# An attention block and two quantised convolutions on one core: a later second convolution, per-chunk statistics, halved first units

## The chip, the cores and the metric

The kernel runs on one core of one Trainium2 chip. The metric is device time in microseconds (us); lower is better. Names such as L1125 are line numbers of the kernel before the change. PE is the matrix engine, DVE the vector engine, ACT the scalar engine, POOL the GpSimd engine, and SP the engine that issues most of the DMAs here.

## The reference, cut to what matters

The input is `x`, 4 images of 128 channels by 128 x 128 pixels, float32. Two layers follow each other.

```python
# layer 0, for each image
tok  = windows of 16x16 pixels, stride 14              # 81 windows
tok  = attention(layernorm(tok) @ w_qkv) @ w_out + b_out + tok
xf   = overlap-average of the windows                   # 128 channels
ym   = layernorm(xf) @ w_p0 + b_p0                      # 256 channels
ym   = depthwise_conv_5x5(ym)
ym   = batchnorm(ym) over images and pixels             # needs every ym first
y    = gelu(gelu(ym)) @ w_p2 + b_p2 + xf                # 128 channels
# layer 1
q    = round(15 * clip(y, 0, 1))
c1   = conv3x3(q, 4-bit w1);  n1 = batchnorm(c1)        # needs every c1 first
q    = round(15 * clip(n1, 0, 1))
c2   = conv3x3(q, 4-bit w2);  n2 = batchnorm(c2)        # needs every c2 first
out  = n2 + y
```

Each of the three batch norms needs the statistics of a whole tensor before its result can be used, so the kernel has four stages with a joint between each two.

## The kernel before, in words

Everything is in one function, `layers`. It is built twice, once for ordinary scores and once (`safe`) under a condition at the end; with these inputs only the first build runs.

**First stage** (to about 2280 us): attention, the first layer norm, the projections and most of the depthwise convolution, in an order of steps written out by hand for the PE, ACT, DVE and SP queues (`tc.manual_schedule`). A planner-free loop over 36 bands of windows puts one band's scores, the next band's layer norm and the previous band's projection beside each other.

**Tail of the depthwise convolution** (`conv_rest`, L644 to L712): the last two row groups of image 3 are convolved in eight chunks of 32 channels, `step(k)` for k from 0 to 7. A chunk is 192 matmuls, two ACT copies out of PSUM (L686), eight `bn_stats` on DVE (L690) and four stores to the DRAM tensor `cv_d`. This call stands outside the hand-made order, so the scheduler of the language puts its instructions in order.

**Depthwise statistics** (L1025 to L1055): 64 `bn_aggr` (L1034) reduce the per-unit statistics `st0` to a mean and a variance per group; a few small DVE operations, eight products with `quad` (L1044) and four one-column matmuls (L1046) add up the partitions; `affine` makes the scale `sc0` and the shift `sh0`. This block too is ordered by the scheduler.

From here on the work goes in 64 *units*: a unit is 8 rows of one image, 1024 pixels, numbered image by image, so that image 3 is units 48 to 63.

**Gelu stage** (`gelu_stage`, from L1148). In step n SP loads unit n+2 (`cv`, 1 MB, then `xfl`, 0.5 MB), ACT does the two gelus of unit n+1 (L1171 twice, L1174), PE does the projection of unit n (L1183, eight matmuls), DVE and POOL make `y`, clip it and quantise it into the padded fp8 image `q1` (L1191, L1195, L1201, L1137), and PE does the first 3x3 convolution of unit n-2 (L1125, 18 matmuls: two halves of 4 rows by 9 taps). DVE takes its statistics (L1133), and ACT copies the result to SBUF (L1207); it goes to DRAM (`c1_d`) except for image 3, which stays in the SBUF tile `c1_s`.

**Second convolution** (`last_stages`, first loop, L1269 to L1287). In step n: ACT scales unit n and applies relu in place (L1277), DVE clips and rounds (L1278) and writes the fp8 integers into `q1` (L1137), PE convolves unit n-2 (L1125), DVE takes its statistics (L1133). For image 3 the result is also copied by ACT into `c1_s` (L1285), in the place from which the unit's input had been read. Each engine takes these in the order of the program, and PSUM has four buffers for results (`ps_d`). At n = 63 the statistics of the units 0 to 59 are aggregated (`most`, L1000), and after the loop the rest (`rest`, L1009).

**Last stage** (L1290 to L1300): the units of images 0 to 2 are convolved a second time, ACT applies the batch norm (L1294), DVE adds `y` (L1295), SP stores the result and loads the next `y`; for image 3 the kept result is used.

Of the kernel before, what the change touches and what calls it, by code (L numbers as in the profile page):

```python
# [8 lines left out]
F32 = mybir.dt.float32  # L9
F8 = mybir.dt.float8e4  # L10
AF = mybir.ActivationFunctionType
# [35 lines left out]
def layers(  # L47
# [49 lines left out]
    c1_d = [dram.tile([P, P * P], F32, name=f"c1_d{b}") for b in range(B - 1)]  # L97
    id_d = [dram.tile([P, P * P], F32, name=f"id_d{b}") for b in range(B)]

    def vector(v, name):  # L100
        n = v.shape[0] // P
        t = const.tile([P, n], F32, name=name)
        nc.sync.dma_start(out=t, in_=v.rearrange("(h p) -> p h", p=P))
        return t

# [27 lines left out]
    with (  # L133
# [36 lines left out]
    st0 = sctx.enter_context(tc.tile_pool(name=f"st0_{tag}", bufs=1)).tile(  # L170
        [P, NCK, 2, 4, len(units), 6], F32, name="st0"
    )


    with ExitStack() as actx:
# [468 lines left out]
        def conv_rest(n, w_t, u_t, c_t):  # L644

            b, g0, ng = units[n]
            early = 5
            at = GR + 2  # L650

            def load(k, a, z, g, m):
                for half in range(2):
                    ch = 32 * k + 16 * half
                    nc.sync.dma_start(
                        out=U[k][64 * half + 2 * a : 64 * half + 2 * z, g : g + m].rearrange(
                            "p g c x -> p g (c x)"
                        ),
                        in_=input_of(b, g0 + g, m, ch, 16, a, z),
                    )  # L660

            U = [u_t.tile([P, ng, 16, CW], F32, name=f"u{k}") for k in range(NCK)]
            W = [w_t.tile([P, 3, 16, 32], F32, name=f"w{k}") for k in range(NCK)]
            for k in range(NCK):
                weights(W[k], k, 0, 2, nc.gpsimd.dma_start)
            for k in range(early):
                load(k, 0, at, 0, 1)

            def late(k):
                if k < early:  # L670
                    load(k, 0, at, 1, 1)
                    load(k, at, GR + 4, 0, ng)
                else:
                    load(k, 0, GR, 0, ng)
                    load(k, GR, GR + 4, 0, ng)

            def step(k):
                sc = ps_s.tile([P, 2, 2, NT], F32, name=f"sc{k % 2}")
                pc = [
                    sc[:, half].rearrange("p a n -> p (a n)").rearrange("p (j g x) -> p j g x", j=4, g=ng)  # L680
                    for half in range(2)
                ]
                depthwise(pc, W[k], U[k], 16)
                for half in range(2):
                    cv = c_t.tile([P, 4, ng, CW], F32, name=f"c{half}")
                    nc.scalar.copy(  # L686
                        cv.rearrange("p j g x -> p (j g x)"), pc[half].rearrange("p j g x -> p (j g x)")
                    )
                    for j in range(4):
                        nc.vector.bn_stats(  # L690
                            st0[:, k, half, j, n, :], cv[:, j].rearrange("p g x -> p (g x)")
                        )
                    engine = (nc.sync, nc.scalar)[half]
                    for g in range(ng):
                        engine.dma_start(
                            out=bass.AP(
                                cv_d[b].tensor,
                                cv_d[b][g0 + g, 32 * k + 16 * half, 0:1].offset,
                                [[CW, P], [4 * GR * P, 4], [1, CW]],
                            ),  # L700
                            in_=cv[:, :, g],
                        )

            def run_all():
                for k in range(4):
                    late(k)
                for k in range(NCK):
                    step(k)
                    if k + 4 < NCK:
                        late(k + 4)  # L710

            return run_all  # L712
# [311 lines left out]

    mv0 = const.tile([P, 2, 2], F32, name="mv0")  # L1025
    with (
        tc.tile_pool(name=f"bn0_{tag}", bufs=1) as bn0,
        tc.tile_pool(name=f"ps_q_{tag}", bufs=1, space=PSUM) as ps_q,
    ):
        nk = NCK * 2 * 4  # L1030
        mv = bn0.tile([P, 2, nk], F32, name="mvp")
        flat = st0.rearrange("p k a j n s -> p (k a j) (n s)")
        for k in range(nk):
            nc.vector.bn_aggr(mv[:, :, k], flat[:, k, :])  # L1034
# [5 lines left out]
        pq = ps_q.tile([P, 2, 2], F32, name="pq")  # L1040
        for m in range(2):
            ex = bn0.tile([P, nk, 4], F32, name=f"ex{m}")
            for q in range(4):
                nc.vector.tensor_scalar(ex[:, :, q], mv[:, m, :], quad[:, q : q + 1], None, ALU.mult)  # L1044
            for h in range(2):
                nc.tensor.matmul(  # L1046
                    pq[:, m, h : h + 1],
                    ex.rearrange("p k q -> p (k q)")[:, h * P : (h + 1) * P], all1,
                    start=True, stop=True,
                )  # L1050
# [4 lines left out]
    sc0, sh0 = affine(mv0[:, 0, :], mv0[:, 1, :], 2, bng, bnb, "0")  # L1055

    sctx.close()

# [89 lines left out]
    def gelu_stage():  # L1148
        with (
# [7 lines left out]
            def load(n):  # L1157
                b, k = units[n]
                cv = ld.tile([P, 2, U], F32, name="cv")
                nc.sync.dma_start(  # L1160
                    out=cv,
                    in_=cv_d[b][k // 2].rearrange("(h p) n -> p h n", p=P)[:, :, pixels(k % 2)],
                )
                xf = ld.tile([P, U], F32, name="xfl")
                nc.sync.dma_start(out=xf, in_=xf_d[b][:, pixels(k)])
                loaded[n] = cv, xf

            def gelus(n):
                cv = loaded[n][0]
                for h in range(2):  # L1170
                    nc.scalar.activation(  # L1171
                        cv[:, h], cv[:, h], AF.Gelu, bias=sh0[:, h : h + 1], scale=sc0[:, h : h + 1]
                    )
                nc.scalar.activation(cv, cv, AF.Gelu)  # L1174

            def second_projection(n):
                b, k = units[n]
# [32 lines left out]

            for n in range(2):
                load(n)
            gelus(0)
            before1()
            before2()
            for n in range(len(units) + 2):
                if n + 2 < len(units):
                    load(n + 2)
                while stores:
# [12 lines left out]
                if n == len(units) - 1:  # L1232
                    most1()
# [5 lines left out]
    def last_stages():  # L1239
        with (  # L1240
# [25 lines left out]
            for n in range(2):  # L1266
                load_first(n)
            sc1, sh1 = rest1()
            for n in range(len(units) + 2):  # L1269
                if n + 2 < len(units):  # L1270
                    load_first(n + 2)
                if n % 4 == 3 and n // 4 < 8:
# [1 line left out]
                if n < len(units):  # L1274
                    b, k = units[n]
                    a = firsts.pop(n)
                    nc.scalar.activation(a, a, AF.Relu, bias=sh1, scale=sc1)  # L1277
                    nc.vector.tensor_scalar(a, a, 15.0, ROUND, ALU.min, ALU.add)  # L1278
                    to_int(rows_in(q1[b], k), a)
                if n >= 2:  # L1280
                    b, k = units[n - 2]
                    pc = conv3x3(ps_d, n - 2, wq[1])
                    stats_of(st2, n - 2, pc)
                    if b == B - 1:
                        nc.scalar.copy(c1_s[:, pixels(k)], pc.rearrange("p h n -> p (h n)"))  # L1285
                if n == len(units) - 1:
# [64 lines left out]
```

## Time and profile before

| what | value |
|---|---|
| time, median of 3 runs | 3292.92 us (3278.27, 3292.92, 3293.81) |
| time of the profiled execution | 3289.4 us |
| its span, first to last instruction | 3287.5 us |
| mean granted PE clock | 0.959 |
| PE busy | 3089.1 us, 94% of the span |
| DVE, ACT, POOL busy | 61%, 61%, 25% |
| DMA moved | 682.75 MB, mean 208 GB/s |
| chain that ended last, PE's share | 76% |

The busy time is summed over the whole span, and the four stages have different limits: in the page's 40 slices PE is at 9 tenths nearly everywhere, and drops to 8, 8 and 4 around 2270 to 2350 us, the tail of the depthwise convolution and its statistics. The question for a change of this sort is therefore not how busy an engine is, but at which places PE waits, and for whom.

### The profile page before, as it was taken

The numbers are of one execution on the slowest core, as the hardware profiler recorded it, in microseconds if no ns is written. First come the engines' busy times: TensorE is split into PE (matmuls) and PEld (weight loads), VectorE is DVE, ScalarE is ACT, GpSimd is POOL, SyncE is SP. The second block draws the span as 40 slices with busy tenths as digits, with TensorE's granted clock in tenths as the row PEclk, the third lists the DMA queues.
The fourth block names the chain that finished last, engine by engine and source line by source line (L and its number), as shares of the span: only waits on it lengthen the run. The fifth ranks groups of instructions, "written<-read, shape, count | busy, mean of one in ns | idle before, by whom it ended". The sixth has DMA issues, their size and how long they took to land.

```text
span 3287.5 us, 75680 instructions
## 1 busy us (share of the span) xinstructions
PE 3089.1 (94%) x30922; PEld 1540.7 (47%) x30922; DVE 2018.0 (61%) x3247; ACT 1989.9 (61%) x2654; POOL 836.3 (25%) x1058
## 2 busy tenths in 40 slices
PE   7999999999999999999999998884899999999998
PEld 3555554544444554444444444553544444444343
DVE  4877887676766667666655564442455555666543
ACT  5777776777777776777656564432477767433443
POOL 3444443333333333333222232211111111000000
PEclk8999999999999999999999998876699999999999
DMA  4555677898886788886888888757899999452398
GB/s 92 133 164 166 173 181 177 195 212 196 204 202 163 192 208 204 195 208 166 190 200 207 202 195 201 192 160 186 256 356 358 358 358 300 150 167 70 101 359 308
DMA packets 810450, 682.75 MB, mean 208 GB/s; under 512 B 581014, under 2 KB 696047, under 8 KB 810095
## 3 DMA queue, kind: packets, MB, share of 16 engines
q1 hardware_dynamic: 799471, 671.26, 75.2%
q8 instruction: 246, 4.03, 0.5%
q0 software_dynamic: 1024, 3.93, 0.5%
q10 hardware_dynamic: 9600, 2.62, 0.4%
q14 instruction: 109, 0.89, 0.1%
HBM read 410.81 MB, written 270.81 MB: 207 GB/s over the span
## 4 chain that ended last, share of the span: by engine, by line
PE 76%; DMA 9%; ACT 5%; issue 4%; DVE 3%; SPq 2%; POOL 0%; ACTq 0%; DVEq 0%; POOLq 0%
PE pc L1125 19%; PE pm L566 9%; PE sc L749 9%; PE po L812 8%; PE pm L459 7%; PE pb L1183 6%; PE pm L527 5%; PE pm L735 4%; PE po L820 3%; DMA y_d<-y 3%; PE pm L358 3%; PE pm L511 3%; DMA u<-y_d 2%; ACT pt L757 1%; DMA xn<-row 1%
## 5 line engine op out<-in xcount | busy, mean ns | idle before, releaser
L832 DVE RECIPROCAL rd<-po 128x256 f32<-128x256 f32 x324 | 569.3, 1757 | 451.6 <-PE po L820 446.5
L1125 PE MATMUL pc<-q,wq 128*128 128x512 fp8e4 x3168 | 701.4, 381 | 14.3 <-DVE q L1137 14.3
L757 ACT ACTIVATE pt<-sc 128x1024 f32<-128x1024 f32 x648 | 627.8, 1024 | 129.1 <-PE sc L749 64.7
L767 POOL TENSOR_TENSOR sm<-pt 128x512 f32<-128x512 f32 x324 | 412.6, 1274 | 1052.8 <-ACT pt L757 748.8
L1125 PEld LDWEIGHTS <-wq 128*128 128x128 fp8e4 x3168 | 308.9, 98 | 417.2 <-issue 49.5
L749 PE MATMUL sc<-q,kr 32*128 32x256 f32 x5184 | 403.6, 414 | 18.9 <-ACT pt L757 18.8
L566 PE MATMUL pm<-u,w 40*32 40x504 f32 (+5 forms) x7680 | 369.2, 504 | 37.2 <-DMA u<-y_d 24.9
L749 PEld LDWEIGHTS sc<-q,kr 32*128 32x128 f32 x5184 | 249.1, 190 | 258.4 <-issue 166.4
L812 PE MATMUL po<-pt,v 128*32 128x256 f32 x5184 | 360.1, 397 | 7.8 <-DVE part L836 7.0
L527 PE MATMUL pm<-xn,wp 128*128 128x512 f32 (+1 forms) x576 | 251.9, 568 | 57.6 <-DVE xn L389 29.4
L613 ACT COPY c<-pm 128x512 f32<-128x512 f32 (+1 forms) x256 | 132.2, 562 | 269.1 <-PE pm L566 257.6
L532 ACT ACTIVATE y<-pm,bp 128x512 f32<-128x512 f32 (+1 forms) x288 | 182.9, 640 | 165.9 <-DMA y_d<-y 86.9
L459 PE MATMUL pm<-xn,wqkv 128*128 128x512 f32 (+1 forms) x576 | 251.9, 566 | 11.2 <-DVE xn L389 7.7
L767 DVE TENSOR_TENSOR sm<-pt 128x512 f32<-128x512 f32 x324 | 243.3, 751 | 27.4 <-ACT pt L757 27.4
L566 PEld LDWEIGHTS pm<-u,w 40*32 40x32 f32 x7680 | 147.0, 112 | 218.7 <-issue 163.5
L617 DVE BATCH_NORM_STATS2 st<-c 128x6 f32<-128x512 f32 (+2 forms) x320 | 160.8, 550 | 138.5 <-ACT c L613 137.9
L1183 PE MATMUL pb<-cv,wp 128*128 128x512 f32 x512 | 231.6, 596 | 6.8 <-ACT cv L1174 6.8
L812 PEld LDWEIGHTS po<-pt,v 128*32 128x32 f32 x5184 | 139.4, 111 | 181.2 <-issue 107.5
L1133 DVE BATCH_NORM_STATS2 st<-pc 128x6 f32<-128x512 f32 x256 | 165.6, 689 | 66.8 <-PE pc L1125 66.8
L820 PE MATMUL po<-sm,ones 128*32 128x256 f32 x2592 | 205.7, 388 | 0.0
L735 PE MATMUL pm<-wqkv,yr 128*128 128x128 f32 x1296 | 193.0, 290 | 0.0
L735 PEld LDWEIGHTS pm<-wqkv,yr 128*128 128x128 f32 x1296 | 158.7, 191 | 68.0 <-issue 44.3
(149 smaller groups left out, 3424.9 us busy)
## 6 DMA issues: line engine op xcount, KB each, us to landing
cv<-cv_d SPq DMA_DIRECT2D x64, 1024.0 KB
u<-y_d SPq DMA_DIRECT2D x230, 256.0 KB
cv_d<-c SPq DMA_DIRECT2D x192, 256.0 KB
xn<-row SPq DMA_DIRECT2D x80, 512.0 KB
y_d<-y SPq DMA_DIRECT2D x160, 256.0 KB
xfl<-xf_d SPq DMA_DIRECT2D x64, 512.0 KB
id_d<-y SPq DMA_DIRECT2D x64, 512.0 KB
idt<-id_d SPq DMA_DIRECT2D x64, 512.0 KB
```

The costliest lines, as they stand in the source:

```text
L459: nc.tensor.matmul(pm[:, : n * P], wqkv[:, m * P : (m + 1) * P], held["xn"][hh], start=True, stop=True,)
L527: nc.tensor.matmul(pm[:, : n * P], wp0[:, h, :], held["xn"][hh], start=True, stop=True)
L566: nc.tensor.matmul(outs[half][32 * q : 32 * q + 32, j, :, a:z], wt[hs, s, c, :], ut[hs, :, c, a + s - 1 : z + s - 1], start=(s == 1), stop ...
L735: nc.tensor.matmul(pv[:, m, c, :], region(yr, j + m)[:, c * P : (c + 1) * P], wqkv[:, 2 * P :], start=True, stop=True,)
L749: nc.tensor.matmul(sc[h // 2][:, h % 2, kc, :].rearrange("p (r c) -> p r c", c=RS), region(kr, j)[hs, kc * P : (kc + 1) * P], queries(j, h ...
L757: nc.scalar.activation(pt, sc[p], AF.Exp)
L767: add(sm, pt[:, :, 0, :], pt[:, :, 1, :], ALU.add)
L812: nc.tensor.matmul(po[hs, 0, :], v[:, kc, hs], pt[h // 2][:, h % 2, kc, :], start=(kc == 0), stop=(kc == 1),)
L820: nc.tensor.matmul(po[hs, 1, :], ones, sm[h // 2][:, h % 2, :], start=True, stop=True)
L832: nc.vector.reciprocal(rd, po[:, 1, :])
L1125: nc.tensor.matmul(pc[:, h], w[:, t, :], q1[b][:, r + dy : r + dy + RB, dx : dx + P], start=(t == 0), stop=(t == 8),)
L1183: nc.tensor.matmul(pb[:, m], wp2[:, h, :], cv[:, h, px], start=(h == 0), stop=(h == 1))
```

## The change

It has five parts.

1. The small vectors of weights (`vector`, L100) become slices of one tile `vectors` instead of a tile each.
2. The 64 `bn_aggr` are written into the loop of `conv_rest`, eight behind each chunk, and write to a tile `mvp` that is allocated beside `st0`. The statistics block is put under the hand-made order, and its eight products with `quad` become one DVE instruction over 512 elements with repeated operands.
3. The gelus of unit 0 are done in two halves of 512 pixels, each with its three ACT instructions.
4. In the gelu stage the first two loads of `cv` go ahead of the first two loads of `xfl`.
5. In the second convolution the first unit is quantised in two halves of 4 rows, and the convolution of unit n-3 (before: n-2) stands in step n.

```diff
     def vector(v, name):
         n = v.shape[0] // P
-        t = const.tile([P, n], F32, name=name)
+        t = vectors[:, used[0] : used[0] + n]
+        used[0] += n
...
+    def chunk_stats(k):
+        flat = st0[:, k].rearrange("p a j n s -> p (a j) (n s)")
+        for m in range(8):
+            nc.vector.bn_aggr(mvp[:, :, 8 * k + m], flat[:, m, :])
...
                 for k in range(NCK):
                     step(k)
+                    chunk_stats(k)
...
     with (
+        nullcontext() if safe else tc.manual_schedule(engines=MANUAL),
...
-        for k in range(nk):
-            nc.vector.bn_aggr(mv[:, :, k], flat[:, k, :])
...
+        nc.vector.tensor_tensor(
+            mq[1],
+            bass.AP(mq[0].tensor, mq[0].offset, [*mq[0].ap, [0, 4]]),
+            bass.AP(quad.tensor, quad.offset, [quad.ap[0], [0, 2 * nk], quad.ap[1]]),
+            ALU.mult,
+        )
         for m in range(2):
-            ex = bn0.tile([P, nk, 4], F32, name=f"ex{m}")
-            for q in range(4):
-                nc.vector.tensor_scalar(ex[:, :, q], mv[:, m, :], quad[:, q : q + 1], None, ALU.mult)
...
             def gelus(n):
-                cv = loaded[n][0]
-                for h in range(2):
...
-                nc.scalar.activation(cv, cv, AF.Gelu)
+                for px in (slice(0, U // 2), slice(U // 2, U)) if n == 0 else (slice(0, U),):
+                    cv = loaded[n][0][:, :, px]
+                    for h in range(2):
...
+                    nc.scalar.activation(cv, cv, AF.Gelu)
...
             for n in range(2):
                 load(n)
+            for n in range(2):
+                load_xf(n)
...
-            for n in range(len(units) + 2):
+            for n in range(len(units) + 3):
...
-                    nc.scalar.activation(a, a, AF.Relu, bias=sh1, scale=sc1)
-                    nc.vector.tensor_scalar(a, a, 15.0, ROUND, ALU.min, ALU.add)
-                    to_int(rows_in(q1[b], k), a)
-                if n >= 2:
-                    b, k = units[n - 2]
-                    pc = conv3x3(ps_d, n - 2, wq[1])
-                    stats_of(st2, n - 2, pc)
+                    for h in (slice(0, RB), slice(RB, 2 * RB)) if n == 0 else (slice(0, 2 * RB),):
+                        px = slice(h.start * P, h.stop * P)
+                        nc.scalar.activation(a[:, px], a[:, px], AF.Relu, bias=sh1, scale=sc1)
+                        nc.vector.tensor_scalar(a[:, px], a[:, px], 15.0, ROUND, ALU.min, ALU.add)
+                        to_int(rows_in(q1[b], k)[:, h], a[:, px])
+                if n >= 3:
+                    b, k = units[n - 3]
+                    pc = conv3x3(ps_d, n - 3, wq[1])
+                    stats_of(st2, n - 3, pc)
```

More of the change, by code (lines that the diff above doesn't have):

```diff
@@ L98, in layers @@
     id_d = [dram.tile([P, P * P], F32, name=f"id_d{b}") for b in range(B)]
+    vectors, used = const.tile([P, 24], F32, name="vectors"), [0]
     def vector(v, name):
         n = v.shape[0] // P
-        t = const.tile([P, n], F32, name=name)
+        t = vectors[:, used[0] : used[0] + n]
+        used[0] += n
         nc.sync.dma_start(out=t, in_=v.rearrange("(h p) -> p h", p=P))
@@ L169, in layers @@
     sctx = ctx.enter_context(ExitStack())
-    st0 = sctx.enter_context(tc.tile_pool(name=f"st0_{tag}", bufs=1)).tile(
-        [P, NCK, 2, 4, len(units), 6], F32, name="st0"
-    )
+    stp = sctx.enter_context(tc.tile_pool(name=f"st0_{tag}", bufs=1))
+    st0 = stp.tile([P, NCK, 2, 4, len(units), 6], F32, name="st0")
+    mvp = stp.tile([P, 2, NCK * 2 * 4], F32, name="mvp")
+    def chunk_stats(k):
+        flat = st0[:, k].rearrange("p a j n s -> p (a j) (n s)")
+        for m in range(8):
+            nc.vector.bn_aggr(mvp[:, :, 8 * k + m], flat[:, m, :])
     with ExitStack() as actx:
@@ L1030, in layers @@
         nk = NCK * 2 * 4
-        mv = bn0.tile([P, 2, nk], F32, name="mvp")
-        flat = st0.rearrange("p k a j n s -> p (k a j) (n s)")
-        for k in range(nk):
-            nc.vector.bn_aggr(mv[:, :, k], flat[:, k, :])
+        mv = mvp
         sq = bn0.tile([P, nk], F32, name="sqp")
@@ L1040, in layers @@
         pq = ps_q.tile([P, 2, 2], F32, name="pq")
+        ex = bn0.tile([P, 2, nk, 4], F32, name="ex")
+        mq = [mv.rearrange("p m k -> p (m k)"), ex.rearrange("p m k q -> p (m k) q")]
+        nc.vector.tensor_tensor(
[4 more added lines that the diff above has]
+        )
         for m in range(2):
-            ex = bn0.tile([P, nk, 4], F32, name=f"ex{m}")
-            for q in range(4):
-                nc.vector.tensor_scalar(ex[:, :, q], mv[:, m, :], quad[:, q : q + 1], None, ALU.mult)
             for h in range(2):
@@ L1047, in layers @@
                     pq[:, m, h : h + 1],
[L1048 removed]
+                    ex[:, m].rearrange("p k q -> p (k q)")[:, h * P : (h + 1) * P], all1,
                     start=True, stop=True,
@@ L1054, in layers @@
         nc.vector.tensor_tensor(mv0[:, 1, :], mv0[:, 1, :], sq0, ALU.subtract)
-    sc0, sh0 = affine(mv0[:, 0, :], mv0[:, 1, :], 2, bng, bnb, "0")
+        sc0, sh0 = affine(mv0[:, 0, :], mv0[:, 1, :], 2, bng, bnb, "0")
     sctx.close()
@@ L1163, in load, with load_xf @@
                 )
+                loaded[n] = [cv]
+            def load_xf(n):
+                b, k = units[n]
                 xf = ld.tile([P, U], F32, name="xfl")
                 nc.sync.dma_start(out=xf, in_=xf_d[b][:, pixels(k)])
-                loaded[n] = cv, xf
+                loaded[n].append(xf)
             def gelus(n):
-                cv = loaded[n][0]
-                for h in range(2):
[L1171 to L1174, printed above, removed]
+                for px in (slice(0, U // 2), slice(U // 2, U)) if n == 0 else (slice(0, U),):
+                    cv = loaded[n][0][:, :, px]
+                    for h in range(2):
+                        nc.scalar.activation(
+                            cv[:, h], cv[:, h], AF.Gelu, bias=sh0[:, h : h + 1], scale=sc0[:, h : h + 1]
+                        )
+                    nc.scalar.activation(cv, cv, AF.Gelu)
             def second_projection(n):
@@ L1218, in gelu_stage @@
                     load(n + 2)
+                    load_xf(n + 2)
                 while stores:
```

## The prediction

> **What bounds the kernel now.** I read the page's slices first, for where PE falls below 9 tenths; then PE in order of time over those slices; then the chain of waits there.
>
> The slices of the page:
>
> ```profile
> PE   7999999999999999999999998884899999999998
> PEclk8999999999999999999999998876699999999999
> DMA  4555677898886788886888888757899999452398
> ```
>
> Each digit is 82 us. Nothing in the change touches the first 26 slices except where small vectors lie, so look right of the 4 (slice 29): the statistics block and the start of the gelu stage. Then the second convolution in order of time, on PE (start, length, work, idle before it and who ended it):
>
> ```profile
> 2809.98 11.88 PE L1125 MATMUL pc<-q,wq 128*128 128x512 fp8e4 x54
> 2827.88 212.53 PE L1125 MATMUL pc<-q,wq 128*128 128x512 fp8e4 x969 [6.02 <-DVE q L1137]
> 3041.25 4.07 PE L1125 MATMUL pc<-q,wq 128*128 128x512 fp8e4 x18 [0.83 <-DVE q L1137]
> 3046.15 4.07 PE L1125 MATMUL pc<-q,wq 128*128 128x512 fp8e4 x18 [0.83 <-DVE q L1137]
> ...
> 3080.43 4.07 PE L1125 MATMUL pc<-q,wq 128*128 128x512 fp8e4 x18 [0.83 <-DVE q L1137]
> 3085.33 14.92 PE L1125 MATMUL pc<-q,wq 128*128 128x512 fp8e4 x68 [0.83 <-DVE q L1137]
> ```
>
> PE is unbroken to 3040 and then waits once per unit for DVE. The chain of waits from 3015 to 3092 shows why; here is one round of it:
>
> ```profile
> 3027.79 1.01 ACT c_s L1285
> 3028.80 1.15 ACT c_s L1277
> 3029.95 0.02 issue
> 3029.97 0.70 DVE c_s L1278
> 3030.68 0.02 issue
> 3030.70 0.70 DVE q L1137
> 3031.40 1.21 DVE st L1133 x2
> ```
>
> This is a ring without PE: statistics, copy to `c1_s`, relu of the next unit (behind the copy in ACT's queue), rounding, integers, and then the next statistics (behind them in DVE's queue). One round is 4.90 us (3032.69 less 3027.79, the next copy's start), while PE needs 3.91 for 18 matmuls. So image 3 costs PE 0.99 us a unit: ten gaps from 3041 to 3085, 9.9 us.
>
> The other two places, first DVE in the convolution's tail and then ACT at the gelu stage's start:
>
> ```profile
> 2328.84 1.65 DVE L690 BATCH_NORM_STATS2 st<-c 128x6 f32<-128x128 f32 x8 [3.16 <-ACT c L686]
> 2330.39 1.54 DVE L1034 BATCH_NORM_AGGREGATE mvp<-st 128x2 f32<-128x36 f32 x8
> ```
>
> ```profile
> 2343.40 2.37 ACT L1171 ACTIVATE cv<-cv,shift,scale 128x1024 f32<-128x1024 f32 x2 [1.82 <-DVE shift L980]
> 2345.80 1.91 ACT L1174 ACTIVATE cv<-cv 128x2048 f32<-128x2048 f32 x1
> ```
>
> The first pair decides part 2: the eight `bn_aggr` already follow each chunk's `bn_stats`, because the scheduler had placed them there. In the second, PE's first projection starts at 2347.77, on gelu 0. From 2373.43 PE never waits until the stage's end.
>
> **What the Trainium skill says.** *PSUM — Partial Sum Buffer*, Terms: two engines on one bank and quadrant at once collide, reads against reads included. That is why a copy waits for statistics that read the same result; the trace agrees (statistics end 3027.70, copy starts 3027.79). *TensorE: Matmul & The Clock Gate*, Architectural detail: ACT and DVE are strictly first in, first out, which closes the ring above. The same page, Part 1: after idling PE runs at half clock for about 3.4 us of work; here the granted clock is 0.50 from 2348 to 2350, 0.82 in the next 2 us and then 1.00. *VectorE: DVE Perf Modes*, The TRN2 errata: each operation pays a fixed cost, and a float32 `tensor_tensor` takes (N+151)/0.96 ns, 0.69 us for 512; L389 has 0.688 for that shape.
>
> **Part by part.**
>
> *Vectors in one tile.* The same 13 DMAs in the same order; the two programs have the same instructions and waits on every engine of the first stage. 0.
>
> *Statistics by chunk, and the products.* 64 `bn_aggr` of 0.27 us stay where they are: 0. Eight products leave (start 2338.22 to end 2339.77, PE starting on the first four at 2339.27) and one of 512 elements comes, 0.69 us by L389. It cannot start before the last correction of `mvp` ends (2338.61), so it ends near 2339.40, and PE's first column matmul is 0.1 to 0.2 later. The four matmuls (1.84 us) then run as before. I take **+0.2 us**, bounds -0.5 (the second pair used to wait, and no longer does) and +0.4.
>
> *Gelu 0 in halves, `cv` loads first.* ACT's price for half sizes is not in the trace. From 1.229 us for 1024 elements (L1171), 1.911 for 2048 (L1174) and 1.054 for 1024 (L352) the slope is about 0.84 us per 1024, and a constant stays with each instruction. A half then takes about 0.80, 0.80 and 1.06 us, overlapping as now: 2.65 us until PE may start, 5.0 for both halves against 4.22 now. So projection 0 starts near 2346.1, 1.6 sooner. It still runs at half clock, but its ramp is over sooner, and it ends near 2351.2 instead of 2352.8. The load of unit 3 (SP, 2352.99) waits for just that, with the DMA engines idle from 2351 to 2354; it, the `xfl` load and the store of `y` 0 behind it on SP move up by as much. Against that, gelus 1 and 2 end 0.8 later, and projection 2, which waits for gelu 2 (2356.18), with them. Which of the two wins? PE's last wait of this start, 1.36 us before projection 4 at 2373.43, hangs on `y` 2 waiting for the store of `y` 0 (DVE, 1.87 us, until 2362.80), then quantisation 2, statistics 0, copy 0 and gelu 4. With the store 1.6 sooner, `y` 2 follows projection 2 (2360.6), gelu 4 ends near 2371.3, and PE, unbroken from projection 2, reaches projection 4 at 2371.9: **-1.5 us**. Bounds +0.9 (only ACT's delay) and -2.5 (half instructions dearer by nothing). The reordered loads are 0: all of them had landed by 2350.5. Beyond 2373 the gain lasts, since PE runs unbroken.
>
> *Quantisation 0 in halves.* Relu starts at 2825.13, PE at 2827.88, after 1.25 + 0.70 + 0.70 us and releases. In halves: relu 0.81, rounding and integers 0.42 each by the fixed cost above, so PE starts near 2826.9. The first six matmuls of a half-unit need rows 0 to 3 only, the seventh (2828.2) row 4, which is ready at 2827.7; unit 1, at 2829.3, comes before its first reader (2830.1). **-1.0 us**, bounds 0 and -1.2.
>
> *Three units behind.* PE's order is unchanged; statistics and copies move one step back in DVE's and ACT's queues. The ring stays: relu n+1 stands behind copy n-3, copy n-3 behind statistics n-3, those behind integers n. The round is still 4.90. What changes is where it begins: copy 48 is now in front of relu 52, not 51, while the convolution of unit 48 ends at the same time. The integers of unit 63 thus come eleven rounds later instead of twelve, 4.90 us sooner, and 9.9 - 4.9 = 5.0 us of waiting remain. **-4.9 us**, bounds 0 and -9.9. Behind it on DVE: the aggregation at n = 63 (3.7 us) now stands before three units' statistics, not two, so the last scale comes 1.3 us later relative to PE. PSUM's four buffers hide that: the first reconvolution needs the buffer of unit 60, free by then, and the fifth that of the first z, ready some 8 us before.
>
> *The last stage.* PE is full, DMA nearly so, over 3150 to 3200:
>
> ```profile
> 3150.00:3200.00 50.00, 50.00 (x232) 22.46 (x231) 21.51 (x18) 20.51 (x18) 0.00 (x0) 1.00 0.99 357
> ```
>
> (Length, then PE, PEld, DVE, ACT and POOL busy, clock, DMA share, GB/s.) The last two groups load nothing, so DMA is at 0.44 from 3270 to 3280, and a backlog drains: the end follows PE.
>
> Sum: +0.2 - 1.5 - 1.0 - 4.9 = **-7.2 us**. The profiled execution took 3289.4 us, 1.9 around its span, and would become 3282.2; the median of the three runs is 3.5 above it, so I forecast 3292.9 - 7.2 = **3285.7 us**. That is 0.22%; about 0.5% (16 us) is what a measurement of this kernel can tell from no change.
>
> **The rivals.**
>
> *The stall of image 3 goes altogether*, if one more unit of lead is enough. Then the term is -9.9, the time 3280.7. For it: PE's waits are short, 0.83 us. Against it: the ring doesn't contain PE, so a lead is used up at 0.99 us a unit.
>
> *The starts don't pay*: the DMA engines (share 1.00, 360 GB/s over 2400 to 2500) or ACT's longer halves take back what the first units gain. Then +0.9, 0, -4.9 and +0.2: 3289.1. For it: that share. Against it: PE doesn't wait in there.
>
> *The statistics part does nothing*: that is in my sum already, by the two lines shown.
>
> *Slower: the addresses move.* `vectors` shrinks and `mvp` grows the pools before those of attention, so every tile after them may lie elsewhere. If that made the exponentials (L757, 648 of 1.024 us) dearer, PE, which waits 18.8 us for them already, would wait more. From 11 ns each (7.2 us) it decides; at 3%, 31 ns, it is +20, and the time 3305.8. Against it: no instruction there changes shape, and no row shows a dependence on place.
>
> **How the numbers follow.** My forecast 0.55; the stall gone 0.13; the starts not paying 0.22; the slower rival 0.10. The terms' bounds give gains from 0 to 14, and the three runs spread over 15.5 us by themselves, so a median may lie 10 either way: 3269 to 3297. Faster by over 0.5% needs below 3276.5: 0.13, most of it from the second case and a low median. Slower: 0.08. Within: 0.79.
>
> **What would show it.** In the profile after: L1034's successor still eight behind each chunk; ACT's first gelu about 0.8 us long; PE's first projection some 2.7 us after ACT's first gelu starts (now 4.4), and projection 4 28.5 us after it (now 30.0); about five gaps of 0.8 instead of ten before the reconvolution; copy to copy still 4.90. Wrong would be ten gaps or none, a projection 4 over 30 us after that start, or a group of attention with another mean.

## The result and the profile after

Medians of 20 runs each on one chip: **3290.51 us** after the change (3279.0 to 3299.5) and 3294.39 us before (3278.3 to 3304.9). The ratio is 0.9988, with an interval of [0.9975, 1.0001]: 3.9 us less, between 8.2 less and 0.3 more, not told apart from no change. The forecast was 7.2 us less.

The profiled execution took 3293.49 us, with a span of 3291.7 us, which is 4.2 more than in the profile before. The slices of its page:

```profile
PE   7999999999999999999989998874799999999998
PEclk8999999999999999999999998877699999999999
```

They look nearly as before, with the smallest digit of PE in the same slice. In the profile before, the digits 8, 8, 8 and 4 cover 1972 to 2301 us, and the 4 alone 2219 to 2301, earlier than the 2270 to 2350 us given further up. It is not the convolution's tail that makes it small: PE waits there 29.41 us for the last layer norm (L389) and 8.35 us for a DMA. The change touches neither wait.

A span hides what happened, because it adds two differences of opposite sign. So I cut it at one event, the start of ACT's first gelu:

| | before | after | difference |
|---|---|---|---|
| start to first gelu (first stage, statistics) | 2343.40 | 2354.27 | +10.87 |
| first gelu to end ("late span") | 944.10 | 937.43 | -6.67 |

The late span is nearly what was forecast. The first row is no measure of the change: single executions of either kernel differ by over 20 us. The second convolution of the kernel after, on PE in order of time (start, length, work, idle before it and who ended it):

```profile
2837.56 231.71 PE L1139 MATMUL pc<-q,wq 128*128 128x512 fp8e4 x1059 [5.05 <-DVE q L1151]
3070.10 4.07 PE L1139 MATMUL pc<-q,wq 128*128 128x512 fp8e4 x18 [0.83 <-DVE q L1151]
...
3089.69 70.68 PE L1139 MATMUL pc<-q,wq 128*128 128x512 fp8e4 x325 [0.83 <-DVE q L1151]
```

Five gaps of 0.83 us are left of ten (3070 to 3090), and the wait ahead of this convolution is 5.05 us instead of 6.02. One round of the ring, from the chain of waits after:

```profile
3037.05 1.01 ACT c_s L1311
3038.06 1.15 ACT c_s L1303
3039.23 0.70 DVE c_s L1304
3039.96 0.70 DVE q L1151
3040.66 1.21 DVE st L1147 x2
...
3041.95 1.01 ACT c_s L1311
```

Copy to copy it is still 4.90 us. (L1311, L1303, L1304, L1151, L1147 are the old L1285, L1277, L1278, L1137, L1133.) The joint and the gelu stage's start after the change, first DVE, then ACT, then PE:

```profile
2347.21 1.54 DVE L181 BATCH_NORM_AGGREGATE mvp<-st 128x2 f32<-128x36 f32 x8
...
2349.30 0.69 DVE L1052 TENSOR_TENSOR ex<-mvp,quad 128x512 f32<-128x512 f32 x1
```

```profile
2354.27 1.52 ACT L1191 ACTIVATE cv<-cv,shift,scale 128x512 f32<-128x512 f32 x2 [1.99 <-DVE shift L991]
2355.82 1.06 ACT L1194 ACTIVATE cv<-cv 128x1024 f32<-128x1024 f32 x1
```

```profile
2356.93 10.41 PE L1203 MATMUL pb<-cv,wp 128*128 128x512 f32 x16 [3.06 <-ACT cv L1194]
...
2384.07 3.70 PE L1203 MATMUL pb<-cv,wp 128*128 128x512 f32 x8 [1.28 <-ACT cv L1194]
```

PE at the same two places before:

```profile
2347.77 12.12 PE L1183 MATMUL pb<-cv,wp 128*128 128x512 f32 x24 [4.76 <-ACT cv L1174]
...
2373.43 3.70 PE L1183 MATMUL pb<-cv,wp 128*128 128x512 f32 x8 [1.36 <-ACT cv L1174]
```

The product (L1052) takes the 0.69 us that was used for it. A half takes 0.76 us for each of the two gelus with scale and shift and 1.06 us for the second gelu, and PE starts 2.66 us after the first gelu instead of 4.37. But projection 4 (2384.07) comes 29.80 us after it, where 30.03 was before and 28.5 was forecast.

Two questions remain: whether the first stage takes longer, although no instruction in it was changed, and why PE's earlier start brought only 0.2 us.

### The profile page after: what moved, and what is told of

It reads as the page before. It is cut to its first block, busy times and chain, and to the rows that moved or that the text cites. A ratio compares the mean times of both kernels' runs of the same rounds, so it can differ in the third digit from the quotient of the medians.

```text
span 3291.7 us, 75680 instructions
## 1 busy us (share of the span) xinstructions
PE 3091.6 (94%) x30922; PEld 1539.0 (47%) x30922; DVE 2018.1 (61%) x3242; ACT 1991.5 (61%) x2658; POOL 837.5 (25%) x1058
## 3 DMA queue, kind: packets, MB, share of 16 engines
q0 software_dynamic: 1024, 3.93, 0.5%
## 4 chain that ended last, share of the span: by engine, by line
PE 76%; DMA 8%; ACT 5%; issue 4%; SPq 4%; DVE 3%; POOL 0%; ACTq 0%; DVEq 0%; POOLq 0%
PE pc L1139 19%; PE sc L760 9%; PE pm L576 9%; PE po L823 8%; PE pm L469 7%; PE pb L1203 6%; PE pm L537 5%; PE pm L746 4%; PE po L831 3%; PE pm L368 3%; PE pm L521 3%; DMA y_d<-y 2%; DMA u<-y_d 2%; ACT pt L768 2%; DMA xn<-row 1%
## 5 line engine op out<-in xcount | busy, mean ns | idle before, releaser
L768 ACT ACTIVATE pt<-sc 128x1024 f32<-128x1024 f32 x648 | 628.1, 1024 | 128.4 <-PE sc L760 64.3
L542 ACT ACTIVATE y<-pm,vectors 128x512 f32<-128x512 f32 (+1 forms) x288 | 182.8, 641 | 167.3 <-DMA y_d<-y 84.2
L469 PE MATMUL pm<-xn,wqkv 128*128 128x512 f32 (+1 forms) x576 | 252.8, 567 | 11.2 <-DVE xn L399 7.6
L1147 DVE BATCH_NORM_STATS2 st<-pc 128x6 f32<-128x512 f32 x256 | 165.4, 689 | 61.8 <-PE pc L1139 61.8
```

What stands on the lines that cost most here:

```text
L469: nc.tensor.matmul(pm[:, : n * P], wqkv[:, m * P : (m + 1) * P], held["xn"][hh], start=True, stop=True,)
L768: nc.scalar.activation(pt, sc[p], AF.Exp)
```

## The experiments

Each group of kernels ran on one chip together with the kernel before, and ratios are to that. The chips differ: the medians of the kernel before were 3291.17, 3288.32, 3281.19 and 3275.78 us in the four groups. In what follows "old places" are the addresses in SBUF that the tiles of attention have in the kernel before. The change moves them up by 192 bytes a partition: 13 small tiles that took 32 bytes each become one of 96, which gives back 320, and `mvp` takes 512 ahead of them.

### First group: the parts by themselves

**lag_only**: the kernel before, with the second convolution three units behind and nothing else.

```diff
-            for n in range(len(units) + 2):
+            for n in range(len(units) + 3):
...
-                if n >= 2:
-                    b, k = units[n - 2]
-                    pc = conv3x3(ps_d, n - 2, wq[1])
-                    stats_of(st2, n - 2, pc)
+                if n >= 3:
+                    b, k = units[n - 3]
+                    pc = conv3x3(ps_d, n - 3, wq[1])
+                    stats_of(st2, n - 3, pc)
```

> The kernel before, with only the second convolution moved from two to three units behind its quantisation. Measure: from the start of the first gelu (the first L1171) to the end of the span, 944.1 us before and 937.4 us in the changed kernel. Ring theory (statistics, copy, relu, rounding, integers go round in 4.90 us; the lead saves exactly one round): 939.2 us, five gaps of 0.83 us on PE before the last stage. Rival 1 (a unit of lead is enough, the changed kernel's remaining gaps come from another part): no gaps, 934.2 us. Rival 2 (the gain in the second convolution came from the halved first unit alone): ten gaps, 944.1 us. Total time about 5 us under the kernel before, inside its spread.

Ratio 0.9987 [0.9978, 0.9996], 4.3 us less. Five gaps, as the ring theory had it; late span 939.38, so 4.72 less. The part does alone what the forecast gave it (4.9).

**four_behind**: the kernel after, with the same lines at n - 4.

> The changed kernel with the second convolution four units behind instead of three. Ring theory: one more round of 4.90 us saved, so of the 5.0 us of waiting next to nothing is left: no gap or one small one, 932.5 us from first gelu to end (937.4 in the changed kernel). Rival (PSUM has four result buffers, and a result is now released one unit later): PE waits for buffers instead, gaps named DVE st or ACT c_s, 937 us or more.

Ratio 0.9984 [0.9974, 0.9995]. PE over the end of the second convolution:

```profile
2833.00 244.88 PE L1139 MATMUL pc<-q,wq 128*128 128x512 fp8e4 x1116 [5.06 <-DVE q L1151]
3078.57 4.07 PE L1139 MATMUL pc<-q,wq 128*128 128x512 fp8e4 x18 [0.70 <-ACT c_s L1311]
3083.47 4.07 PE L1139 MATMUL pc<-q,wq 128*128 128x512 fp8e4 x18 [0.83 <-ACT c_s L1311]
3088.49 71.77 PE L1139 MATMUL pc<-q,wq 128*128 128x512 fp8e4 x330 [0.96 <-ACT c_s L1311]
```

The gaps that waited for integers are gone, and three others have come: they end with a copy out of PSUM. With four results under way, the four buffers of `ps_d` are full, and PE waits for the oldest to be read. The first two of them still follow the ring, because the copies that free PSUM come at its pace: they start at 3072.61, 3077.51 and 3082.41.

From this convolution's start to the end the time falls from 454.14 (after) to 452.90, 1.24 us instead of the 4.9 that one more round would give, so the rival had the mechanism. The late span, 934.64, lies between the two forecasts (932.5, and 937 or more), but 1.55 us of its gain come from an earlier start of this convolution, which PE's clock explains (see warm_after); at its own beginning it lost some 1.0 us to the clock, which stayed at half for 5.21 us here and for 3.27 in the kernel after. DVE shows what made the last gap the longest:

```profile
3082.35 3.40 DVE L1011 BATCH_NORM_AGGREGATE mv<-st 128x2 f32<-128x720 f32 x1
...
3086.06 4.87 DVE L1147 BATCH_NORM_STATS2 st<-pc 128x6 f32<-128x512 f32 x8
```

The long aggregation stands ahead of four units' statistics, and with them of the copies: the next one starts at 3087.43, 5.02 us after the one before instead of 4.90.

**relu_ahead**: the kernel after, with the relu of unit n+1 issued ahead of the copy of unit n-3.

```diff
...
+            relu(0)
             for n in range(len(units) + 3):
...
-                        nc.scalar.activation(a[:, px], a[:, px], AF.Relu, bias=sh1, scale=sc1)
...
+                    if n + 1 < len(units):
+                        relu(n + 1)
                 if n >= 3:
```

> The changed kernel, three units behind, but the relu of unit n+1 is issued on ACT before the copy of unit n-3. Ring theory: the copy now holds up only the relu after next, so one round serves two units, 2.45 us a unit against PE's 3.91, and PE has no gap: 932.4 us from first gelu to end. Rival (DVE or ACT simply have too much work per unit in image 3, or the copy's wait for the statistics is the limit): gaps of 0.8 us as before, 937.4 us. In total about 12 us under the kernel before (0.36%), if the first stage is alike.

Ratio 0.9979 [0.9968, 0.9990]. One row holds the whole second convolution and the beginning of its repetition:

```profile
2825.23 334.94 PE L1139 MATMUL pc<-q,wq 128*128 128x512 fp8e4 x1530 [5.06 <-DVE q L1151]
```

and ACT's copies now come at PE's pace, 3.91 us apart:

```profile
3032.70 1.01 ACT L1319 COPY c_s<-pc 128x1024 f32<-128x1024 f32 x1 [1.75 <-DVE st L1147]
...
3036.61 1.01 ACT L1319 COPY c_s<-pc 128x1024 f32<-128x1024 f32 x1 [1.75 <-DVE st L1147]
```

Late span 932.30; 932.4 was expected. That it fits so closely is luck in part: this convolution started 1.16 us sooner than in the kernel after, and from its start to the end it saved 3.97 us where 5.0 were expected. PE's clock would account for both (see warm_after for the half a microsecond per microsecond): it stayed at half for 5.67 us from this start here and for 3.27 us in the kernel after, and half of the difference, 1.20 us, makes up what the 3.97 lack. What shows the cause is that the gaps are gone, all five. So the ring made the gaps, and the order of two instructions in ACT's queue closed it (queues strictly in order, as the Trainium skill has it in *TensorE: Matmul & The Clock Gate*, Architectural detail).

**addresses**: the kernel before, with the packed vectors and `mvp` beside `st0`, and nothing else of the change.

```diff
+    vectors, used = const.tile([P, 24], F32, name="vectors"), [0]
...
-        t = const.tile([P, n], F32, name=name)
+        t = vectors[:, used[0] : used[0] + n]
+        used[0] += n
...
+    mvp = stp.tile([P, 2, NCK * 2 * 4], F32, name="mvp")
...
-        mv = bn0.tile([P, 2, nk], F32, name="mvp")
+        mv = mvp
```

> The kernel before with only the small vectors in one tile and the statistics tile allocated early, which is what may move the places of the attention's tiles. If places don't matter: the first gelu starts where it does in the kernel before within its spread (2343 there, 2354 in the one execution of the changed kernel), 944.1 us from there to the end, ratio 1.000. If places matter (the slower rival of the prediction): the first stage longer by some 5 us or more, ratio 1.002 or above, and the mean of a large group of the attention (L757 1.024 us, L832 1.757 us) changed by over 1%.

Ratio **1.0021 [1.0012, 1.0031]**: 6.9 us more (4.7 by the medians), with the same instructions in the same order on every engine and a late span of 945.19. The mean of L757 is 1.024 us here too, so the other half of that expectation, a large group of attention with another mean, didn't come. This part, costed at nothing, costs about what the late edits gain.

### Second group: is it the place?

**pad192**: the kernel before with an unused tile of 192 bytes a partition in the pool of `st0` (`stp`). **vec_pad320**: the packed vectors, and an unused tile of 320 bytes that puts the tiles of attention back to the old places.

```diff
+    spare = stp.tile([P, 192 // 4], F32, name="spare")     # vec_pad320: 320 // 4
+    nc.vector.memset(spare[:, :1], 0.0)
```

> The kernel before with one unused tile of 192 bytes a partition beside st0: the attention stage's tiles stand 192 bytes higher, just where part 1 and the early mvp of the change put them, and nothing else differs (constants, statistics, orders as before; one memset of a column is added before the first stage). Theory (the place of the attention tiles costs the first stage some 5 to 6 us, as the kernel with the packed vectors and the early mvp suggested with its ratio of 1.0021): ratio near 1.0018, so some 5 us over the kernel before, with the span from the first gelu to the end still 944 to 945. Rival A (not their place but that of the packed vectors, which every evacuation reads as a bias): no difference, ratio 1.000 with an interval that holds 1. Rival B (the 1.0021 was chance): no difference either, and then none in the run with packed vectors and a pad.

> The kernel before with the small vectors in one tile (part 1 of the change) and an unused tile of 320 bytes a partition beside st0, which puts the attention stage's tiles back where the kernel before has them; the statistics stand as before. Theory (the place of the attention tiles): ratio 1.000, within 2 us of the kernel before. Rival A (the packed vectors themselves): ratio near 1.0018, some 5 us more. Rival B (chance): 1.000 here and in the run with the pad of 192 bytes.

Ratios 1.0014 [1.0003, 1.0024] and 0.9997 [0.9984, 1.0010]. The unused tile of 192 bytes alone makes the kernel slower; the packed vectors, with the old places restored, don't. It is the place of the later tiles that counts.

**best**: relu_ahead's late edits on the old places, with the old vectors and the old statistics block (the diffs are those of the change's parts 3 to 5 and of relu_ahead).

> The kernel before, with its tiles and its statistics block untouched (every tile of the attention stage at its old address), and three late edits: first gelu in halves with the cv tiles loaded first, first quantisation in halves, second conv three chunks behind, and the relu of chunk n+1 put ahead of the copy of chunk n-3. Theory (the first stage pays for the address shift, the late stages gain): the late span 944.1 falls to 932.1 or so, as in the run with the relu ahead (932.30, of which the statistics block is no part after the first gelu), and with no first-stage cost the total is some 12 us under the kernel before, ratio near 0.9964. Rival (no address cost; the late gain is partly given back elsewhere): ratio 0.998, as the run with the relu ahead on the changed kernel's tiles had it.

Ratio **0.9958 [0.9941, 0.9975]**, 13.6 us less, late span 931.51. The rival's 0.998 is outside the interval. It beats the kernel before; the kernel after (0.9988, on another chip) has an interval that meets this one at 0.9975. Relu_ahead's 0.9979 is this times the 1.0021 of addresses, which is closer than the intervals can vouch for.

**warm_after**: the kernel after with idle matmuls ahead of the first projection.

```diff
+            idle = ps_c.tile([P, 2, RB * P], F32, name="pc")
+            for _ in range(4):
+                nc.tensor.matmul(idle[:, 0], ident, loaded[0][1][:, : RB * P], start=True, stop=True)
             gelus(0)
```

> The changed kernel with four idle matmuls of 128x512 put on PE ahead of the first projection (they read ident and the first xf tile, and their result is used by nobody), so that PE is at work some microseconds before the first gelus end. Theory (what ate the gelu halves' gain in the changed kernel's profile is that PE stayed at half clock for 6 us after its first projection): the granted clock is 1.00 by the second projection at the latest, projection 4 starts 28.5 us after the first gelu (29.8 in the changed kernel's profile) and the second conv starts 481.7 to 482.2 after it (483.3). Rival (the loads hold the projections): projection 4 stays at 29.8 and the second conv at 483.3 whatever the clock.

This one missed: the idle matmuls read the first `xfl` tile, which lands late now that the `cv` tiles are loaded first; they waited 4.00 us for it, took 5.46 us themselves, and held the projection up. PE:

```profile
2355.33 5.46 PE L1237 MATMUL pc<-xfl,ident 128*128 128x512 f32 x8 [4.00 <-DMA xfl<-xf_d]
```

The first projection started 8.89 us after the first gelu, and the second convolution 486.28. It says nothing on the question. What does is a comparison of the profiles (the windows from 2 to 4 and from 4 to 6 us after the first projection's start; the clock is that granted to PE, as a share of full speed; columns are length, then PE, PEld, DVE, ACT and POOL busy, clock, DMA share, GB/s), of the kernel after:

```profile
2358.93:2360.93 2.00, 2.00 (x4) 0.88 (x3) 0.00 (x0) 2.00 (x3) 2.00 (x8) 0.50 0.88 352
2360.93:2362.93 2.00, 2.00 (x3) 0.68 (x2) 0.00 (x0) 1.97 (x2) 0.84 (x2) 0.50 0.16 64
```

and of four_behind, which has the same gelu stage:

```profile
2355.92:2357.92 2.00, 2.00 (x5) 0.92 (x4) 0.00 (x0) 2.00 (x3) 2.00 (x8) 0.75 0.86 344
2357.92:2359.92 2.00, 1.17 (x3) 0.19 (x1) 0.79 (x2) 1.97 (x2) 0.85 (x2) 1.00 0.11 43
```

The granted clock stayed at 0.50 for 6.0 us after PE's start in the one, and for 3.0 us in the other. PE on the first and the last of four_behind's projections of this start:

```profile
2353.92 5.17 PE L1203 MATMUL pb<-cv,wp 128*128 128x512 f32 x8 [3.06 <-ACT cv L1194]
...
2379.62 3.59 PE L1203 MATMUL pb<-cv,wp 128*128 128x512 f32 x8
```

In windows of 0.2 us, over the twelve profiles without idle matmuls, with times counted from the first gelu:

| gelu 0 | clock full at (us) | second convolution starts at (us) |
|---|---|---|
| whole (before, lag_only, vec_pad320, pad192, addresses, pad320) | 7.37, 7.76, 7.97, 8.17, 8.96, 8.97 | 484.48, 484.52, 484.65, 484.75, 485.34, 485.21 |
| in halves (four_behind, relu_ahead, best, late_only, after_pad128, after) | 5.66, 6.46, 7.46, 8.06, 8.26, 8.66 | 481.74, 482.13, 482.62, 482.83, 482.98, 483.29 |

Within a row, each microsecond of half clock goes with half a microsecond of the second convolution's start. From this follows an estimate for projection 4, from the profiles' own numbers. In halves PE works 1.71 us longer before that point, at half clock, which is worth 0.86 us. In the kernel after the clock was full 1.3 us later than in the kernel before (8.66 against 7.37), which takes 0.65 back: 0.2 us are left, and 0.23 was measured (29.80 against 30.03). In four_behind it was full 1.7 us sooner, which adds 0.86: 1.7 us, and 1.67 was measured (28.36 against 30.03). The other four in halves fit to 0.2 us.

Between the rows, the means differ by 2.2 us (484.83 and 482.60), of which 0.97 belongs to the quantisation in halves (5.05 against 6.02). That leaves 1.3 us for the gelu halves on the mean of six and six profiles, and 0.2 in the kernel after's own.

### Third and fourth group: closing the sum

**late_only**: best without the relu ahead, that is, the change's parts 3 to 5 on the old places.

> The changed kernel without its first two parts: small vectors in tiles of their own and the statistics block as before, so that every tile of the attention stage has its old address; the gelu halves, the cv-first loads, the quantisation halves and the second conv three chunks behind stay. Theory (the late edits gain what was forecast and the address shift of the first two parts ate about half of it): from the first gelu to the end 936.5 to 938 (937.43 in the changed kernel, 944.10 before), and with no first-stage cost ratio near 0.9978, some 7 us under the kernel before. Rival (the late gain does not reach the total, whatever the addresses): ratio 0.9988, as the changed kernel had it.

Ratio 0.9966 [0.9951, 0.9981], late span 937.15. The interval holds the 0.9978 of the theory and not the rival's 0.9988, but it is 11.2 us less where the late span gave 7.0. Times the 1.0021 of addresses it is 0.9987; the whole change had 0.9988, a closer fit than the intervals can vouch for.

**pad320**: as pad192, with 320 bytes.

> The kernel before with an unused tile of 320 bytes a partition beside st0 instead of 192: the attention stage's tiles 320 bytes up. It asks whether any shift costs or only that of the change. Theory A (a shift off the old places costs about the same, 4 to 6 us): ratio 1.0012 to 1.0018. Theory B (it depends on the place): a ratio clearly under or over that, 1.000 or less included.

Ratio **0.9985 [0.9977, 0.9994]**: Theory A, with 1.0012 or more, is outside the interval, so it is not any shift that costs; it matters where the tiles come to stand. Whether this place is better than the old one is less sure than the ratio looks (see the table of rests below).

**best_warm**: best with two idle matmuls that read a tile that is ready in time.

```diff
             nc.tensor.matmul(pq, all1, mask, start=True, stop=True)
+            idle = ps_p.tile([P, 2 * P], F32, name="idle")
+            for _ in range(2):
+                nc.tensor.matmul(idle, all1, sq, start=True, stop=True)
```

> The kernel with the three late edits and the relu ahead on the old tiles, and two idle matmuls of 128x256 put on PE behind the last small matmul before the gelu stage (they repeat the one on sq and nobody uses their result), so that PE works from about 0.4 us ahead of the first gelu instead of from 2.66 us after it. Theory (the start of the second conv follows the moment at which PE leaves its half clock, by half a us for each us, as the profiles so far have it: 5.66, 6.46, 7.46, 8.66 us after the first gelu went with 481.74, 482.13, 482.62, 483.29; PE leaves it 3.0 to 6.0 us after it began to work): the clock is full 2.6 to 5 us after the first gelu, the second conv starts 480.2 to 481.4 after it, and the total is 1 to 2 us under that kernel (ratio to the kernel before near 0.9953). Rival (the clock only goes along with something else, such as the cv transfers): the second conv stays at 481.7 to 483.3.

Ratio 0.9943 [0.9924, 0.9962], which its few runs (6) don't tell apart from best; late span 931.67, against 931.51 in best, so none of the 1 to 2 us expected. PE in order of time:

```profile
2333.40 2.06 PE L1087 MATMUL idle<-sq,all 128*128 128x256 f32 x4
2336.59 1.98 PE L1192 MATMUL pb<-cv,wp 128*128 128x512 f32 x4 [1.14 <-ACT cv L1183]
2339.10 1.98 PE L1192 MATMUL pb<-cv,wp 128*128 128x512 f32 x4 [0.52 <-ACT cv L1183]
2343.30 3.70 PE L1192 MATMUL pb<-cv,wp 128*128 128x512 f32 x8 [2.22 <-ACT cv L1183]
```

The clock was full 1.6 us after the first gelu, sooner than the 2.6 to 5 expected, and so for the whole first projection: each half takes 1.98 us, where the eight matmuls took 6.05 in best. But the second convolution starts at 481.86, later than the 480.2 to 481.4 of the theory and within the rival's range, and no sooner than with the clock full at 5.66 (481.74). So this run doesn't confirm that the clock is the cause. It fits it in one way: PE now waits 2.22 us for ACT, and projection 4 starts 28.36 us after the first gelu, as in four_behind, so from there on the gelus set the time and a sooner clock has nothing left to give. That reading was made after the run. The 0.77 us by which this convolution starts sooner than in best were lost again at its own beginning, where the clock stayed at half for 4.45 us, against 2.68 in best.

**after_pad128**: the whole change, with an unused tile of 128 bytes that makes its shift 320 bytes.

> The changed kernel, whole, with one unused tile of 128 bytes a partition beside st0: the attention stage's tiles stand 320 bytes above their old places instead of 192. Theory (the first stage's time depends on where its tiles stand: 192 bytes up cost 1.0014 and 1.0021, 320 bytes up gave 0.9985, and the late edits' gain comes on top): ratio near 0.9985 x 0.9967 = 0.995, and not over 0.997, with the span from the first gelu to the end as before at 936.5 to 938. Rival (the shift is not what the changed kernel pays for): 0.9988 as without the unused tile.

Ratio 0.9971 [0.9958, 0.9983], late span 937.07. That is under the 0.9988 of the change as it was, as the theory wants, though the two intervals overlap and the chips differ. It is over the 0.995 expected, and just over the 0.997 that was named as the limit: the extra gain of pad320 didn't show on top.

For all kernels, the total (from the ratio) less the change of the late span, with 0.17 us added for the new statistics block where it is in, leaves what the first stage did (the total is from many executions, the late span from one):

| place of attention's tiles | kernel: total, late part, rest (us) |
|---|---|
| old | lag_only -4.3, -4.7, +0.4; vec_pad320 -1.0, +0.2, -1.2; best -13.8, -12.6, -1.2; late_only -11.2, -7.0, -4.2; best_warm -18.7, -12.4, -6.3 |
| 192 bytes up | after -4.0, -6.5, +2.5; four_behind -5.3, -9.3, +4.0; relu_ahead -6.9, -11.6, +4.7; addresses +6.9, +1.1, +5.8; pad192 +4.6, +0.6, +4.0 |
| 320 bytes up | pad320 -4.9, +1.2, -6.1; after_pad128 -9.5, -6.9, -2.6 |

Each rest is uncertain by 3 to 6 us, but all five at 192 are positive, and all but one of the others negative. The kernels of one group share a chip and their runs of the kernel before, so a comparison within a group is safer. In the first group the three at 192 lie 3.6 to 5.4 us above the one at the old places, and in the second pad192 lies 5.2 above the two at the old places. In the third, late_only and best_warm stand at the old places and have -4.2 and -6.3 all the same, which no run explains. Pad320's -6.1 lies between theirs. So the runs show that 192 bytes cost; that 320 bytes are better than the old places they don't show.

## Why the prediction was right, and where it was not

Against the kernel before on the same chip the change made 3.9 us less, where 7.2 less was forecast; the direction, and that it is too small to tell from no change, were as said. The time itself, 3290.51 us, is 4.8 us over the 3285.7 forecast, 1.5 of it because the kernel before had 3294.39 over 20 runs and 3292.92 over three; the range of 28 us, made for the spread of single runs, would have held no gain at all as well. What speaks for the working is not that range, but the late span: 6.67 us less, where its terms (-1.5, -1.0 and -4.9) made 7.4. By the steps of the prediction:

- *Statistics by chunk, and the products, +0.2.* Last `bn_aggr` to first gelu went from 5.35 to 5.52 us: +0.17. The aggregations stand eight behind each chunk, as before. Right.
- *Quantisation 0 in halves, -1.0.* The wait ahead of the second convolution fell from 6.02 to 5.05 us. Right.
- *Three units behind, -4.9.* Five gaps instead of ten at a round of 4.90 us. From the second convolution's start to the end, the time fell from 459.62 to 454.14, 5.5 us in these two profiles, some 0.4 of it from a shorter stretch of half clock at this start (3.27 us against 4.12); lag_only alone took 4.7 off the late span. Right, with its reason: relu_ahead, which opens the ring, has no gap at all. The rival in which the stall goes altogether fell; a fourth unit of lead did not bring it either, because PSUM's buffers come next.
- *Gelu 0 in halves, -1.5.* It was 0.2 in the kernel after's profile, and 1.3 on the mean over profiles. The step that failed is "its ramp is over sooner": the half clock lasted 3.0 us of PE's work in the profile before, and I took a length near that as fixed, although the page that the prediction cites for the clock (*TensorE: Matmul & The Clock Gate*, Part 1) also says that the moment varies from run to run. It lasted 6.0 in the profile after, so the load of unit 3 was issued 9.41 us after the first gelu (9.59 before) and next to nothing moved up. Where it lasted 3.0, in four_behind, that load came at 7.91 and projection 4 at 28.36 us, and the forecast had said 28.5. The mechanism was right, and the size hangs on something that varies from run to run. That the clock itself causes the delay, rather than going along with it, rests on the rows of the table and on the estimate below it; best_warm, which was to test it, came out in its rival's range.
- *Vectors in one tile, 0.* Wrong for the whole of parts 1 and 2: their instructions cost next to nothing (the 0.17 us above), but the tiles that they move do. By addresses it is 6.9 us, by pad192 4.6; the rest of the changed kernel, 2.5, agrees but would not show it alone. This step looked at instructions and waits only.
- *The slower rival* named this place and was put at 0.10. Its price was taken from dearer exponentials; their mean is 1024 ns before and after. "A group of attention with another mean" was to show it, and the largest (L757, L832) have the same mean, so the sign that I had chosen was blind to it.

So the sum without addresses is +0.17 - 0.22 - 0.97 - 5.48 = -6.5 us, and the difference to -3.9 would be what the first stage took back. The change's own interval, 8.2 less to 0.3 more, holds -6.5 too; that the places cost anything is shown by addresses and pad192, not by this difference. Late_only, which keeps the old places, had 0.9966 (11.2 us less, the near end of its interval at 6.2).

What stays open is why the place matters. With one profile for each kernel, the first gelu's start shows it badly: in addresses' profile it is at 2344.11, in that of before at 2343.40. The wait of the score matmuls for the exponentials, over 40 to 2200 us, is 18.8 to 23.6 us in six profiles with the old places (mean 21.0), 20.0 to 27.1 in six with 192 bytes (23.2) and 18.5 and 19.6 with 320. These ranges overlap, and the means differ by half of the cost at most. No experiment separated DMA, PE or ACT as the one that feels the place.

## What to carry to other kernels

A change that allocates or packs tiles moves everything behind them, and in a stage that PE nearly fills this was worth about as much as the edits themselves: give such an edit a twin with an unused tile that restores the old addresses, and try one or two other places on purpose. Where a chain of waits closes without the bottleneck engine, more lead only shortens the time for which it bites; find the two instructions in one queue whose exchange opens it. A gain at a stage's start that depends on the clock has to be read from several profiles.

## What the runs showed of the hardware that I had not expected

The same instructions in the same order took 0.14% and 0.21% longer with their tiles 192 bytes higher; with 320 bytes they took no longer.

The half clock of PE lasted from 3.0 to 6.0 us of the first projection's work at the same place in twelve profiles. *TensorE: Matmul & The Clock Gate* of the Trainium skill, Part 1, has a window of about 3.4 us for it that runs freely, so that the moment shifts with where the work begins in it, by some 500 ns either way. The window agrees: within each trace, all changes of the granted clock begin on one grid with a step of 3.413 us (the half clock before the first projection's end lasted 71.68 us, 21 steps, in the profile before). The 500 ns don't: the moment moved over 3.1 us, nearly a whole step.

That half clock was older than the pause before the projection. In the profile before it began at 2279 us, in PE's wait of 8.35 us, and lasted through the whole tail of the depthwise convolution: 1536 matmuls from 40 partitions, with PE busy for 44.28 of 49.02 us, all at 0.50. Being busy was not enough there to bring the full clock back; 3.0 us of the first projection, from 128 partitions, were. No run tells which property of those matmuls makes the difference.
